# A graph network on one core: node rows spread from 32 nodes of a chunk instead of 128, one edge projection for k and v, sums joined per window

## The chip, the cores and the metric

The kernel runs on one core of a Trainium2 chip. Its time is the device time of one execution in microseconds; the median of 11 executions is 7646.16 us (7627.25 to 7656.26). The engines named below are PE (matrix products, with PEld for its weight loads), DVE (vector), ACT (scalar), POOL (GpSimd, here the issuer of the gathers) and SP (the issuer of most other DMAs).

## What is computed

A graph of 6,250 nodes and 206,250 edges, sorted by target node. First one message layer: each edge takes its target's features and 16 edge features, and the node averages the messages. Then three attention layers over the same edges with 32 edge features. Cut to the core:

```python
# message layer, on h = relu(layernorm(x))
msg  = relu(concat(h[dst], edge_attr_16) @ W1 + b1)
x    = x + relu(segment_sum(msg, dst) / max(count, 1) + h @ Wres + bres)
# three attention layers, starting from h = relu(layernorm(x)); two heads of 32, two of 32, one of 64
q, k, v = h @ Wq + bq, h @ Wk + bk, h @ Wv + bv
e     = edge_attr_32 @ We                       # the same e for k and for v
alpha = sum(q[dst] * (k[src] + e)) / sqrt(C)
a     = softmax of alpha over the edges of one dst
h     = segment_sum(a * (v[src] + e), dst) + h @ Ws + bs   # PReLU after the first two
# at the end x + h
```

## The kernel before

The edges are padded to 404 chunks of 512 (`CH`); a window is four chunks, 2,048 edges in 16 tiles of 128, and there are 101 windows (`NW`). Because edges are sorted by target, a window touches at most 128 neighbouring nodes, counted from its first node (`base`). A check of the target list at the start chooses between this program (`windows`) and a general one that handles any list; with these inputs `windows` runs.

*Spreading a node's row to its edges.* PE multiplies a transposed one-hot (`ohT`, 128 nodes by the edges of a tile, bf16) with the rows of the window's 128 nodes. To keep 32-bit precision the rows are cut into three bf16 parts (`parts`), and there are three matmuls for each tile that add up in PSUM.

*Summing edges into nodes.* PE multiplies a one-hot (`oh`, edges by 128 nodes, f32, made on DVE by comparing a row of indices with the edge's local node `dl`) with the messages, into one PSUM tile `acc` per window. The first node of a window can be the last of the window before; a matmul with `last` as weights adds the earlier window's sum of it (L339, L532).

*The graph stage* (L302 to L366) goes window by window: it loads edge features (eight DMAs for four windows, L311), the local node numbers (`lb`, L315) and the node rows (`q`, L317), makes `ohT` on DVE and also writes it to DRAM (`ohd`, L321) for the layers; projects the edges (L325), spreads the rows (L329), applies the activation (L333), makes one-hots (L336), sums (L340), and then normalises the nodes and projects them for the first attention layer (`project`), which stores k and v (L261), q with the skip row (L262) and the node features (L352).

*A layer* (`attention`) goes chunk by chunk. `fetch` (L383) gathers the k and v rows of 512 edges by four indirect DMAs on POOL, four chunks ahead. `load` brings a window's edge features (four DMAs, L391), its `ohT` and its `q`, one window ahead. `scores` projects the edges (L415, 512 columns: e stands twice, for k and for v), spreads q (L419, 12 matmuls of a chunk), adds e to k and v (L421), multiplies (L423) and reduces (L425). When a group of four windows (`ST` = 64 tiles) has its scores, `rows`, `chain` and `columns` find the maxima by scans and the exponentials. `sums` follows some 18 chunks behind: weights times v (L524), one-hots (L529), sums (L533), and at the end of a window `done` divides, adds the skip row and calls `project` for the next layer. What is left of `sums` after a layer's last gather is called the drain below; the gathers of the next layer need all of its k and v rows.

*Order.* A scheduler orders the instructions of each engine; each engine then works in that order. A DMA whose DRAM address depends on a window's first node needs a register load from SBUF on SP first (`first_node`, L234). The DMAs of SP and ACT take eight completion semaphores in turn, and an issue waits until the DMA that had its semaphore before has landed. Most pools have two or three buffers; PSUM tiles two.

Of the kernel before, what the change touches and what calls it, by code (L numbers as in the profile page):

```python
# [30 lines left out]
P = 128  # L31
# [15 lines left out]
WC = WT // 4  # L47
NR = NP + P
# [5 lines left out]
QW = 96 + D  # L54
# [10 lines left out]
def gnn_kernel(ctx: ExitStack, tc: tile.TileContext, x, src_t, dst_t, dst_row, ea16, ea32, eaT16, eaT32, w, out):  # L65
# [25 lines left out]
    base_i = cp.tile([1, NW], I32, name="base_i")  # L91
    base = cp.tile([P, NW], F32, name="base")
    with tc.tile_pool(name="chk", bufs=1) as p, tc.tile_pool(name="chkp", bufs=1, space=PSUM) as pp:
# [4 lines left out]
        ends = p.tile([NW, 2], F32, name="ends")  # L98
# [3 lines left out]
        nc.vector.tensor_copy(ends[:, 0:1], cur[:, 0:1])  # L102
        nc.vector.tensor_copy(ends[:, 1:2], after)
        nc.vector.memset(ends[0:1, 0:1], 0.0)
        bad = p.tile([NW, 2], F32, name="bad")
        fall = p.tile([NW, WE], F32, name="fall")
        nc.vector.tensor_tensor(fall, prev, cur, op=OP.is_gt)
        nc.vector.tensor_reduce(bad[:, 0:1], fall, axis=AX.X, op=OP.add)
        span = p.tile([NW, 1], F32, name="span")
        nc.vector.tensor_sub(span, ends[:, 1:2], ends[:, 0:1])  # L110
        nc.vector.tensor_single_scalar(bad[:, 1:2], span, float(P - 1), op=OP.is_gt)
        ones = p.tile([NW, P], F32, name="ones")
        nc.vector.memset(ones, 1.0)
        pb = pp.tile([P, NW], F32, name="pb")
        nc.tensor.matmul(pb, ends[:, 0:1].to_broadcast([NW, P]), ident[:NW, :NW], start=True, stop=True)
        nc.vector.tensor_copy(base, pb)
        nc.vector.tensor_copy(base_i, pb[0:1, :])
        pbad = pp.tile([P, 2], F32, name="pbad")
# [6 lines left out]
        nc.vector.tensor_scalar(lb, cur, ends[:, 0:1], None, op0=OP.subtract)  # L125
# [13 lines left out]
def windows(ctx: ExitStack, tc, x, src_t, dst_t, eaT16, eaT32, w, out, ident, w0, wl, slope, lrow, starts, base_i,  # L139
# [6 lines left out]
    qt = [dr.tile([NR, QW + D if l == 0 else QW], F32, name=f"qt{l}") for l in range(LAYERS + 1)]  # L146
# [3 lines left out]
    ohd = dr.tile([NW, P, WE], BF16, name="ohd")  # L150
# [10 lines left out]
    pidx = iota([P, 1], "pidx", [[0, 1]], 1)  # L161
    one = cp.tile([1, P], F32, name="one")
# [19 lines left out]
    for l in range(LAYERS):  # L182
        t = cp.tile([P, 8 * D], F32, name=f"wblk{l}")
        nc.gpsimd.memset(t, 0.0)
        for j in range(4):
            for i in range(2):
                nc.scalar.dma_start(t[j * 32:(j + 1) * 32, (2 * j + i) * D:(2 * j + i + 1) * D], w[f"L1_gnn_We{l}"])
        wblk.append(t)
    srci = cp.tile([P, T], I32, name="srci")
    nc.sync.dma_start(srci, src_t)  # L190

    dl = cp.tile([P, NW, WT], F32, name="dl")
    step = cp.tile([P, NW], F32, name="step")
    last = cp.tile([P, NW], F32, name="last")
    nc.vector.tensor_sub(step[:, :NW - 1], base[:, 1:], base[:, :NW - 1])
    nc.vector.tensor_scalar(last[:, :NW - 1], step[:, :NW - 1], pidx[:, 0:1], None, op0=OP.is_equal)
    with tc.tile_pool(name="dsti", bufs=1) as p:
        dsti = p.tile([P, NW, WT], I32, name="dsti")
        nc.sync.dma_start(dsti, dst_t.rearrange("p (w t) -> p w t", t=WT))
        nc.vector.tensor_tensor(dl, dsti, base[:, :, None].to_broadcast([P, NW, WT]), op=OP.subtract)  # L200
# [32 lines left out]
    def first_node(wi):  # L233
        return nc.values_load(base_i[0:1, wi:wi + 1], engines=(SP,), min_val=0, max_val=NP,  # L234
                              skip_runtime_bounds_check_because="a node")

    def parts(wp, q, dest):

        k = len(q.shape) - 1
        at = lambda i: dest[(slice(None),) * k + (slice(i * D, (i + 1) * D),)]  # L240
# [6 lines left out]
    def project(wp, mp, h, l, wi):  # L247
# [9 lines left out]
        q = wp.tile([P, QW], F32, name="q_n")  # L257
        parts(wp, po[:, :D], q[:, :96].bitcast(BF16))
        nc.scalar.copy(q[:, 96:], po[:, 3 * D:])
        at = first_node(wi)  # L260
        nc.sync.dma_start(kvt[l + 1][bass.ds(at, P), :], kv)  # L261
        nc.sync.dma_start(qt[l + 1][bass.ds(at, P), :], q)  # L262


    with tc.tile_pool(name="n0", bufs=1) as pool, tc.tile_pool(name="n0w", bufs=2) as wp, \
# [17 lines left out]
        rows = pool.tile([P, NB + 1, QW + D], F32, name="rows")  # L283
        nc.gpsimd.memset(rows[:, NB, :], 0.0)
        nc.gpsimd.tensor_copy(rows[:, :NB, QW:], xs)
        for b0 in range(0, NB, 4):
# [10 lines left out]
            parts(wp, po[:, :nb, :D], rows[:, b0:b0 + nb, :96].bitcast(BF16))  # L297
            nc.vector.tensor_copy(rows[:, b0:b0 + nb, 96:QW], po[:, :nb, D:])
        nc.sync.dma_start(qt[0].rearrange("(b p) f -> p b f", p=P), rows)


    with tc.tile_pool(name="g0", bufs=2) as gp, tc.tile_pool(name="e0", bufs=3) as ep, \  # L302
# [3 lines left out]
        for wi in range(NW):  # L306
# [7 lines left out]
            lb = gp.tile([P, WE], BF16, name="lb0")  # L314
            nc.sync.dma_start(lb, lrow[None, wi * WE:(wi + 1) * WE].to_broadcast([P, WE]))  # L315
            q = gp.tile([P, QW + D], F32, name="q0")
            nc.sync.dma_start(q, qt[0][bass.ds(first_node(wi), P), :])  # L317
            qb = q[:, :96].bitcast(BF16)
            ohT = gp.tile([P, WE], BF16, name="ohT0")
            nc.vector.tensor_scalar(ohT, lb, pidx[:, 0:1], None, op0=OP.is_equal)  # L320
            nc.scalar.dma_start(ohd[wi], ohT)  # L321
            acc = pp.tile([P, D + 1], F32, name="acc0")
            for u in range(2):
                pm = pp.tile([P, 8 * D], F32, name="pm")
                nc.tensor.matmul(pm, ea[:, wi % 4, u, :], w0blk, start=True, stop=False)  # L325
                for j in range(8):
                    t = u * 8 + j
                    for s in range(3):
                        nc.tensor.matmul(pm[:, j * D:(j + 1) * D], ohT[:, t * P:(t + 1) * P], qb[:, s * D:(s + 1) * D],  # L329
                                         start=False, stop=(j == 7 and s == 2))  # L330
# [3 lines left out]
                oh = ep.tile([P, 8, P], F32, name="oh0")  # L334
                for j in range(8):
                    nc.vector.tensor_scalar(oh[:, j, :], row, dl[:, wi, u * 8 + j:u * 8 + j + 1], None, op0=OP.is_equal)  # L336
                for j in range(8):
                    if wi > 0 and u == 1 and j == 7:
# [808 lines left out]
```

## Time and profile before

| | us |
|---|---|
| median of 11 executions | 7646.16 |
| profiled execution, its own time | 7659.01 |
| its span, first to last instruction | 7657.0 |
| PE busy (share of the span) | 5775.8 (75%) |
| POOL busy | 4756.8 (62%) |
| DVE busy | 4230.1 (55%) |
| ACT busy | 908.7 (12%) |
| mean granted PE clock | 0.733 |
| mean share of the DMA engines | about 0.35 in the layers, 0.43 in the graph stage |

Stages by the trace: start until 219 us, graph stage 219 to 1265, first gather at 1277.5, layers to 3340.3, 5469.3 and 7596.8 (last gather's end), each followed by a drain of 60 to 68 us. In the views, a group's line has the line of the code, the engine, the operation, out<-in with shapes and the count, then busy us and the mean ns of one, then the engine's idle us just before them and what ended most of that. A timeline's line has start us, duration us, engine (SPq and ACTq are DMA issues), line, operation and count, and in brackets the idle time before and its releaser. A line of waits has total us, times and the longest.

### The profile page before, as it was taken

How to read it: one execution, taken by the hardware profiler on the slowest of the kernel's cores; microseconds unless marked ns; L12 is line 12 of the kernel's file. 1: busy time of each engine (PE TensorE's matmuls, PEld its weight loads, DVE VectorE, ACT ScalarE, POOL GpSimd, SP SyncE). 2: the span in 40 equal slices, each digit the busy share in tenths (PEclk: the TensorE clock that was granted, in tenths of full speed). 3: DMA queues.
4: the chain of work that ended last, by engine and by line, in shares of the span. 5: the costliest groups of instructions: out<-in, count | busy, mean ns of one | idle time of the engine just before them, and what ended most of it. 6: DMA issues, size and time to landing. Idle time of an engine off the chain costs nothing. (4 is left out here: it accounts for less than half of the span.)

```text
span 7657.0 us, 121925 instructions
## 1 busy us (share of the span) xinstructions
PE 5775.8 (75%) x38234; PEld 4059.7 (53%) x38234; DVE 4230.1 (55%) x16431; ACT 908.7 (12%) x4161; POOL 4756.8 (62%) x5246
## 2 busy tenths in 40 slices
PE   1898887777777877776787777778767778777777
PEld 1676665555555555454554555555545555555555
DVE  2565455555555555554555555555545555555555
ACT  1232221011111111110111111111100000000000
POOL 0000002777777777747777777777477777777775
PEclk9998887677766677856768777776666776666676
DMA  1543434333333333323333333333233333333332
GB/s 34 184 158 129 137 129 124 99 101 103 101 104 101 100 104 102 101 71 100 100 105 101 102 103 101 104 102 100 70 100 97 101 97 98 99 96 98 99 96 73
DMA packets 680405, 789.19 MB, mean 103 GB/s; under 512 B 256945, under 2 KB 536851, under 8 KB 679517
## 3 DMA queue, kind: packets, MB, share of 16 engines
q1 hardware_dynamic: 507928, 408.61, 17.6%
q0 software_dynamic: 155136, 318.03, 14.8%
q10 hardware_dynamic: 16687, 54.66, 1.9%
q8 instruction: 309, 5.06, 0.3%
q14 instruction: 345, 2.83, 0.1%
HBM read 669.72 MB, written 112.64 MB: 102 GB/s over the span
## 5 line engine op out<-in xcount | busy, mean ns | idle before, releaser
L383 POOL DMA_INDIRECT kv<-kvt,srci x4848 | 4687.9, 967 | 1511.2 <-issue 1164.3
L415 PE MATMUL pe<-wblk,ea 128*128 128x512 f32 x2424 | 2008.3, 923 | 1355.2 <-DVE kv L421 1287.6
L533 PE MATMUL acc<-u,oh 128*128 128x66 f32 (+1 forms) x9696 | 2145.0, 359 | 138.2 <-DVE oh L529 106.1
L421 DVE TENSOR_TENSOR kv<-kv,pe 128x512 f32<-128x512 f32 x1212 | 832.0, 687 | 2401.7 <-DMA kv<-kvt,srci 2113.2
L533 PEld LDWEIGHTS acc<-u,oh 128*128 128x128 f32 x9696 | 1884.4, 267 | 251.5 <-DVE oh L529 113.1
L419 PEld LDWEIGHTS <-ohT 128*128 128x128 bf16 x14544 | 1004.1, 127 | 1074.2 <-issue 867.3
L415 PEld LDWEIGHTS pe<-wblk,ea 128*128 128x128 f32 x2424 | 495.3, 254 | 1501.2 <-DVE kv L421 1254.7
L529 DVE TENSOR_SCALAR oh<-row,dl 128x128 f32<-128x128 f32 x4848 | 1126.4, 290 | 8.4 <-PE acc L533 8.2
L419 PE MATMUL pq<-q,ohT 128*128 128x64 bf16 x14544 | 1028.5, 226 | 14.8 <-DMA q<-qt 10.3
L332 POOL MEMSET msg<- 128x8 f32 x202 | 22.7, 113 | 1039.3 <-PE acc L340 899.5
L524 DVE TENSOR_TENSOR u<-kv,ex 128x256 f32<-128x256 f32 x1212 | 505.4, 417 | 5.5 <-issue 2.9
L336 DVE TENSOR_SCALAR oh<-row,dl 128x128 f32<-128x128 f32 x1616 | 380.1, 281 | 232.2 <-PE acc L340 196.7
L425 DVE TENSOR_REDUCE al<-prod 128x8 f32<-128x256 f32 (+1 forms) x1212 | 497.6, 411 | 1.3
L423 DVE TENSOR_TENSOR prod<-kv,pq 128x256 f32<-128x256 f32 x1212 | 493.7, 408 | 5.2 <-DVE kv L421 0.5
L340 PEld LDWEIGHTS acc<-msg,oh 128*128 128x128 f32 x3232 | 429.7, 205 | 107.9 <-issue 73.0
L523 ACT COPY u<-ex 128x8 f32<-128x8 f32 (+1 forms) x1212 | 235.1, 201 | 2113.7 <-PE acc L533 2095.8
L340 PE MATMUL acc<-msg,oh 128*128 128x65 f32 x3232 | 455.0, 290 | 29.6 <-ACT msg L333 13.7
L325 PE MATMUL pm<-w0blk,ea 128*128 128x512 f32 x404 | 253.8, 725 | 25.9 <-DMA ea<-in_eaT_dram 25.9
L254 PE MATMUL po<-wl,ht 65*128 65x256 f32 x606 | 247.9, 497 | 8.4 <-ACT ht L252 8.0
L329 PEld LDWEIGHTS <-ohT 128*128 128x128 bf16 x4848 | 188.0, 103 | 94.5 <-issue 68.3
L329 PE MATMUL pm<-q,ohT 128*128 128x64 bf16 x4848 | 191.8, 198 | 43.6 <-DMA q<-qt 40.1
L552 ACT COPY win<-acc 128x66 f32<-128x66 f32 (+1 forms) x303 | 65.3, 215 | 1311.2 <-PE acc L533 1308.2
(156 smaller groups left out, 2988.5 us busy)
## 6 DMA issues: line engine op xcount, KB each, us to landing
ohT<-ohd SPq DMA_DIRECT2D x303, 512.0 KB
ea<-in_eaT_dram SPq DMA_DIRECT2D x1412, 64.0 KB
kv<-kvt,srci POOLq DMA_INDIRECT x4848
lb<-lrow SPq DMA_DIRECT2D x101, 512.0 KB
ohd<-ohT ACTq DMA_DIRECT2D x101, 512.0 KB
qt<-q_n SPq DMA_DIRECT2D x303, 80.0 KB
kvt<-kv_n SPq DMA_DIRECT2D x303, 64.0 KB
q<-qt SPq DMA_DIRECT2D x303, 48.0 KB
```

The costliest lines, as they stand in the source:

```text
L329: nc.tensor.matmul(pm[:, j * D:(j + 1) * D], ohT[:, t * P:(t + 1) * P], qb[:, s * D:(s + 1) * D], start=False, stop=(j == 7 and s == 2))
L336: nc.vector.tensor_scalar(oh[:, j, :], row, dl[:, wi, u * 8 + j:u * 8 + j + 1], None, op0=OP.is_equal)
L340: nc.tensor.matmul(acc, oh[:, j, :], msg[:, j, :], start=(u == 0 and j == 0), stop=(u == 1 and j == 7))
L383: nc.gpsimd.indirect_dma_start(out=t[:, j, :], out_offset=None, in_=kvt[l + 1][:, :], in_offset=bass.IndirectOffsetOnAxis(ap=srci[:, 4 * c ...
L415: nc.tensor.matmul(pe.rearrange("p j f -> p (j f)"), ea[:, k, :], wblk[l], start=True, stop=True)
L419: nc.tensor.matmul(pq[:, j, :], ohT[:, (4 * k + j) * P:(4 * k + j + 1) * P], q[:, i * D:(i + 1) * D], start=(i == 0), stop=(i == 2))
L421: nc.vector.tensor_add(kv, kv, pe)
L423: nc.vector.tensor_mul(prod, kv[:, :, :D], pq)
L425: nc.vector.tensor_reduce(als[s][:, :, t0:t0 + 4].rearrange("p h j -> p j h"), prod.rearrange("p j (h c) -> p j h c", h=H), axis=AX.X, op= ...
L524: nc.vector.tensor_mul(u[:, :, :D].rearrange("p j (h c) -> p j h c", h=H), kv[:, :, D:].rearrange("p j (h c) -> p j h c", h=H), e[:, :, :, ...
L529: nc.vector.tensor_scalar(oh[:, j, :], row, dl[:, wi, 4 * k + j:4 * k + j + 1], None, op0=OP.is_equal)
L533: nc.tensor.matmul(acc, oh[:, j, :], u[:, j, :], start=(k == 0 and j == 0), stop=(k == WC - 1 and j == 3))
```

## The change

In words:

- The node rows are spread from the 32 nodes (`CN`) that a chunk of 512 edges can touch, not from the 128 of a window. The three bf16 parts of these 32 nodes are stacked into 96 partitions, so that one matmul per tile does what three did. The rows of a window are loaded by four DMAs, one per chunk, each with its own first node (`load_q`); `base`, `dl` and the local numbers are kept per chunk.
- The node table is split: bf16 parts (`qt`) and f32 rows for the skip and the residual (`st`), stored and loaded apart.
- The edge projection is done once per chunk, with 256 columns, and added to k and v by one DVE operation that reads it twice.
- The one-hots of the sums have 32 columns and are made by one DVE operation per chunk (in the graph stage one per eight tiles); each chunk's sums go to its own 32 rows of `acc`, and `nodes` joins them per 128 nodes: a copy, a one-hot from `slot`, a matmul and a second copy. The last tile of the first chunk and the carried row are added in the second chunk's turn.
- The edge features of the layers are laid out once, DRAM to DRAM, by four DMAs per window on ACT's queue in the graph stage (`ead`); a layer then loads them by one DMA instead of four.
- `ex` and `sc` have four buffers instead of two.

```diff
+CN = 32
...
+    qt = [dr.tile([NR, 3, D], BF16, name=f"qt{l}") for l in range(LAYERS + 1)]
+    st = [dr.tile([NR, 2 * D if l == 0 else D], F32, name=f"st{l}") for l in range(LAYERS + 1)]
...
+    ohd = dr.tile([NW, 3 * CN, WE], BF16, name="ohd")
+    ead = dr.tile([NW, P, WC, P], F32, name="ead")
...
+    slot = cp.tile([P, NW], F32, name="slot")
+    for c in range(WC):
+        r = slice(c * CN, (c + 1) * CN)
+        nc.vector.tensor_sub(slot[r, :], base[r, :, c], base[r, :, 0])
+    nc.vector.tensor_scalar(slot, slot, pmod[:, 0:1], None, op0=OP.add)
...
         at = first_node(wi)
         nc.sync.dma_start(kvt[l + 1][bass.ds(at, P), :], kv)
-        nc.sync.dma_start(qt[l + 1][bass.ds(at, P), :], q)
+        nc.sync.dma_start(qt[l + 1][bass.ds(at, P)], q)
+        nc.sync.dma_start(st[l + 1][bass.ds(at, P), :], skip)
+
+    def load_q(pool, l, wi):
+        q = pool.tile([3 * CN, WC, D], BF16, name="q")
+        for c in range(WC):
+            at = first_node(wi, c)
+            nc.sync.dma_start(q[:, c, :], qt[l][bass.ds(at, CN)].rearrange("n i f -> (n i) f"))
+        return q
+
+    def nodes(wp, mp, acc, wi, F):
+        s = wp.tile([P, F], F32, name="sums")
+        nc.scalar.copy(s, acc)
+        of = wp.tile([P, P], F32, name="of")
+        nc.vector.tensor_scalar(of, row, slot[:, wi:wi + 1], None, op0=OP.is_equal)
+        pn = mp.tile([P, F], F32, name="pn", tag="m")
+        nc.tensor.matmul(pn, of, s, start=True, stop=True)
+        win = wp.tile([P, F], F32, name="win", bufs=3)
+        nc.scalar.copy(win, pn)
+        return win
...
-        nc.sync.dma_start(qt[0].rearrange("(b p) f -> p b f", p=P), rows)
+        nc.sync.dma_start(qt[0].rearrange("(b p) i f -> p b i f", p=P), q)
+        nc.scalar.dma_start(st[0].rearrange("(b p) f -> p b f", p=P), rows)
...
+            for j in range(4):
+                nc.scalar.dma_start(
+                    ead[wi, j * 32:(j + 1) * 32],
+                    eaT32[:, wi * WE:(wi + 1) * WE].rearrange("k (c j e) -> k c j e", j=4, e=P)[:, :, j])
+            lb = gp.tile([3 * CN, WE], BF16, name="lb0")
+            nc.sync.dma_start(lb, lrow[None, wi * WE:(wi + 1) * WE].to_broadcast([3 * CN, WE]))
+            q = load_q(gp, 0, wi)
+            rx = gp.tile([P, 2 * D], F32, name="rx")
+            nc.sync.dma_start(rx, st[0][bass.ds(first_node(wi), P), :])
...
-                    for s in range(3):
-                        nc.tensor.matmul(pm[:, j * D:(j + 1) * D], ohT[:, t * P:(t + 1) * P], qb[:, s * D:(s + 1) * D],
-                                         start=False, stop=(j == 7 and s == 2))
+                    nc.tensor.matmul(pm[:, j * D:(j + 1) * D], ohT[:, t * P:(t + 1) * P], q[:, t // 4, :],
+                                     start=False, stop=(j == 7))
...
-                oh = ep.tile([P, 8, P], F32, name="oh0")
-                for j in range(8):
-                    nc.vector.tensor_scalar(oh[:, j, :], row, dl[:, wi, u * 8 + j:u * 8 + j + 1], None, op0=OP.is_equal)
+                oh = ep.tile([P, 8, CN], F32, name="oh0")
+                nc.vector.tensor_tensor(oh, row[:, None, :CN].to_broadcast([P, 8, CN]),
+                                        dl[:, wi, u * 8:(u + 1) * 8, None].to_broadcast([P, 8, CN]), op=OP.is_equal)
...
             ea = gp.tile([P, WC, P], F32, name="ea")
-            for j in range(4):
-                nc.sync.dma_start(
-                    ea[j * 32:(j + 1) * 32],
-                    eaT32[:, wi * WE:(wi + 1) * WE].rearrange("k (c j e) -> k c j e", j=4, e=P)[:, :, j])
+            nc.sync.dma_start(ea, ead[wi])
...
-            pe = pp.tile([P, 4, 2 * D], F32, name="pe")
+            pe = pp.tile([P, 4, D], F32, name="pe")
...
-                for i in range(3):
-                    nc.tensor.matmul(pq[:, j, :], ohT[:, (4 * k + j) * P:(4 * k + j + 1) * P], q[:, i * D:(i + 1) * D],
-                                     start=(i == 0), stop=(i == 2))
-            nc.vector.tensor_add(kv, kv, pe)
+                nc.tensor.matmul(pq[:, j, :], ohT[:, (4 * k + j) * P:(4 * k + j + 1) * P], q[:, k, :],
+                                 start=True, stop=True)
+            both = kv.rearrange("p j (i f) -> p j i f", i=2)
+            nc.vector.tensor_add(both, both, pe[:, :, None, :].to_broadcast([P, 4, 2, D]))
...
-            oh = ep.tile([P, 4, P], F32, name="oh")
-            for j in range(4):
-                nc.vector.tensor_scalar(oh[:, j, :], row, dl[:, wi, 4 * k + j:4 * k + j + 1], None, op0=OP.is_equal)
+            oh = ep.tile([P, 4, CN], F32, name="oh")
+            nc.vector.tensor_tensor(oh, row[:, None, :CN].to_broadcast([P, 4, CN]),
+                                    dl[:, wi, 4 * k:4 * k + 4, None].to_broadcast([P, 4, CN]), op=OP.is_equal)
+            if k == 1:
+                if wi > 0:
+                    nc.tensor.matmul(acc[0:1, :], last[:, wi - 1:wi], carried(wi, s, g), start=False, stop=False)
+                nc.tensor.matmul(acc[:CN, :], *state["late"], start=False, stop=True)
             for j in range(4):
-                if wi > 0 and k == WC - 1 and j == 3:
-                    nc.tensor.matmul(acc[0:1, :], last[:, wi - 1:wi], carried(wi, s, g), start=False, stop=False)
-                nc.tensor.matmul(acc, oh[:, j, :], u[:, j, :], start=(k == 0 and j == 0),
-                                 stop=(k == WC - 1 and j == 3))
+                if k == 0 and j == 3:
+                    state["late"] = oh[:, j, :], u[:, j, :]
+                    continue
+                nc.tensor.matmul(acc[k * CN:(k + 1) * CN, :], oh[:, j, :], u[:, j, :], start=(j == 0), stop=(j == 3))
...
-            win = st["win"] = wp.tile([P, F], F32, name="win", bufs=3)
-            nc.scalar.copy(win, acc)
+            win = state["win"] = nodes(wp, mp, acc, wi, F)
```

The graph stage has the same order of sums (`late`, the carried row, 32 rows per chunk) and the same join as the layers.

## The prediction

> **What bounds the kernel now.** I read the engines' busy time by stage first, then the costliest groups, POOL's own timeline, and SP's timeline in the first stage. The views by stage give, for a stretch, each engine's busy us (count), the granted clock, the DMA share and GB/s, in the order PE, PEld, DVE, ACT, POOL:
>
> ```profile
> 219.00:1265.00 1046.00, 900.70 (x8965) 706.27 (x8965) 577.15 (x2894) 282.16 (x998) 22.52 (x199) 0.89 0.43 144
> 1277.50:3340.30 2062.80, 1567.01 (x9634) 1073.56 (x9635) 1201.34 (x4481) 224.74 (x1144) 1574.23 (x1668) 0.72 0.35 102
> 3340.30:3408.00 67.70, 51.74 (x208) 42.92 (x209) 36.77 (x182) 11.51 (x61) 0.85 (x5) 0.53 0.15 36
> ```
>
> The kernel is one graph stage (101 windows, 1046 us, 10.36 us each), three attention layers of about 2061 us, and a drain after each of them (67.7, 67.5 and 60.2 us). In the graph stage PE is busy 86%: PE bounds it. In a layer both PE and POOL show 76%, so busy shares don't decide; the groups and POOL's timeline do.
>
> ```profile
> L383 POOL DMA_INDIRECT kv<-kvt,srci x4848 | 4687.9, 967 | 1511.2 <-issue 1164.3
> L421 DVE TENSOR_TENSOR kv<-kv,pe 128x512 f32<-128x512 f32 x1212 | 832.0, 687 | 2401.7 <-DMA kv<-kvt,srci 2113.2
> L529 DVE TENSOR_SCALAR oh<-row,dl 128x128 f32<-128x128 f32 x4848 | 1126.4, 290 | 8.4 <-PE acc L533 8.2
> ```
>
> ```profile
> 2309.16 0.95 POOL L383 DMA_INDIRECT kv<-kvt,srci  x1 [0.30 <-DVE oh L529]
> 2310.41 0.95 POOL L383 DMA_INDIRECT kv<-kvt,srci  x1 [0.30 <-issue]
> 2311.66 0.95 POOL L383 DMA_INDIRECT kv<-kvt,srci  x1 [0.30 <-issue]
> ...
> 3339.36 0.95 POOL L383 DMA_INDIRECT kv<-kvt,srci  x1 [0.30 <-issue]
> 3395.91 0.30 POOL L451 MEMSET b<- 1x260 f32 x1 [55.61 <-DVE wins L546]
> ...
> 3408.01 0.95 POOL L383 DMA_INDIRECT kv<-kvt,srci  x1 [11.24 <-DMA kvt<-kv_n]
> ```
>
> POOL issues a gather every 1.25 us, with the same 0.30 us between them whoever is named as releaser; it never waits longer inside a layer. 1616 gathers x 1.25 = 2020 us of the layer's 2061. The first DVE work of each chunk waits 2113 us in all for gathers to land, and PE waits for that DVE work. So POOL's gather rate bounds the layers; PE and DVE have slack there. Only in the drains, where POOL is idle, does PE pace again: 38.5 of 67.7 us are the sums of L533.
>
> **The change part by part.**
>
> *Attention, matmuls (L415, L419).* Per chunk the edge projection goes from 512 columns to 256 and the query spread from 12 matmuls to 4: 1004 us of L415 and 8/12 x 1028 = 686 us of L419 leave PE. The gathers cover them; they are worth 0. That cover is not gone anywhere except in the drains, which hold almost none of these rows.
>
> *Attention, one-hots (L529).* Four TENSOR_SCALARs of 290 ns become one TENSOR_TENSOR of the same 128 elements per lane (nearest: 128x128 f32 TENSOR_TENSOR L495, 273 ns); 850 us leave DVE, hidden as well. But the gather itself moves: fastest 941 ns, median 947, mean 967, so 4848 x 20 ns = 97 us lie above the median, and in the undisturbed first 60 us of the second layer, with no L529 running, the rows all show 0.94 or 0.95. Ends: 0 (the new one-hot, or L524, disturbs as much) and -97. I take -60, since L524 runs on unchanged.
> By the Trainium skill, "SBUF — State Buffer", section "Who interferes with whom", a tensor_scalar can lock a port pair that GpSimd needs for its descriptors, while tensor_tensor has no such mode, though with two SBUF inputs it contends with a GpSimd instruction that reads SBUF. By the first half alone the term would be about -97, by the second it could be near 0; the row of 967 against 947 fits either.
>
> *Attention, sums and the new join.* 16 matmuls with 128-wide weights become 16 with 32-wide weights, plus the copy of sums (ACT, as L552, 215 ns), a one-hot (DVE, 290) and one 128-wide matmul and a second copy. Under the gathers: 0. In a drain it counts:
>
> ```profile
> 3392.45 6.64 PE L533 MATMUL acc<-u,oh 128*128 128x66 f32 x30 [0.39 <-ACT u L523]
> 3399.02 0.38 PE L532 MATMUL acc<-wins,last 128*1 128x66 f32 x2
> ```
>
> 30 records take 6.57 us from start to start, 219 ns each; the one with a single weight column takes 155 (3399.02 to 3399.33). A 32-wide one lies between, nearer the latter if loading goes by columns: about 165. A drain holds 160 of them: 160 x 0.054 = 8.6 us less. Against it each of six windows gets two hops more, some 1 us (copy 0.2, join 0.3, copy 0.2 and the handovers), and the row carried from the window before is now wanted in the second chunk instead of the last, so PE, which works in order, has only the six records of the first chunk (1.0 us) to run meanwhile. Net -5 per drain, between 0 and -10; three drains: -15 (0 to -30). The deeper rings for ex and sc can only help here; I give them nothing.
>
> *Start.* The node table goes out as 384-byte rows on SP and 512-byte rows on ACT instead of one 896-byte row: twice the pieces. The old one is issued at 195.84 and lets work begin at 214.4: 18.5 us. Ends: 0 (the same bytes, almost) and +25 (twice the pieces, and other small set-up steps); I take +13.
>
> *Graph stage.* PE loses two thirds of L329 (192 us) and part of L340 (453 us): 128 us and about 453 x (1 - 105/118) = 50 us, where 118 and 105 ns are the start-to-start spacings of wide and single-column sums at full clock. 1046 - 178 leaves 868 us, 8.6 per window: PE stops being alone. DVE loses more than it gets (16 x 280 ns go, two of about 410 and one of 290 come). What is added is issuing. SP's timeline in this stage:
>
> ```profile
> 604.28 0.37 SPq L262 DMA_DIRECT2D qt<-q_n  x1
> 605.17 0.33 SPq L352 DMA_DIRECT2D x1t<-x  x1
> 606.07 0.36 SPq L317 DMA_DIRECT2D q<-qt  x1
> 606.48 0.42 SPq L311 DMA_DIRECT2D ea<-in_eaT_dram  x1
> ```
>
> A DMA whose address is a node read from SBUF comes 0.89 us after the one before; a plain one 0.41 to 0.47. Before, a window has three node reads (q, x1t, kvt) and four plain issues (qt, lb, two of ea): 3 x 0.89 + 4 x 0.45 = 4.5 us. After: seven node reads (four chunks' q, rx, x1t, kvt) and five plain (qt, st, lb, two ea): 6.2 + 2.25 = 8.5 us. That is a floor of 101 x 8.5 = 858 us, about PE's. On top come waits in order on SP:
>
> ```profile
> SPq L261 <- ACT q_n L241: 236.5, 91, 7.4
> SPq L262 <- DVE q_n L245: 79.5, 90, 2.5
> ```
>
> The stores (L261, L262) wait 2.3 and 0.8 us per window; behind them on SP stand the loads for the next windows, for which PE waits. The first mostly vanishes when SP itself is late; the second stays, because L262 follows L261 by 0.4 us and its data need two more steps. I add 0.9 us: 9.4 us per window, 949 us, -97. ACT gets four issues per window for the edge copy (0.43 each by the like loads on SP, L311) and one more copy: 2.8 + 0.33 + 1.7 + 0.2 = 5.0 of 9.4 us. Each issue also waits until the DMA that had its completion semaphore, eight issues back over both queues, has landed (the built program's order shows it); at 17 DMAs per window instead of 8 this ties ACT's computing to SP's pace. Ends: -190 (floors reached, nothing else) and +170 (12 us per window by such ties).
> By the Trainium skill, "DMA: Bandwidth & Descriptors", section "Specifications", pieces under 512 B fall below line rate because of a read-modify-write; the new q rows are 128 B. It gives no price; the trace before has 384-byte q rows only, so nothing here shows it. It speaks for the upper end.
>
> *Sum* against the profiled run's own time: 7659.0 + 13 - 97 - 60 - 15 = 7500. That run is 12.9 us over the median of the eleven shown, so 7490 on their scale.
>
> **The rivals** (on the median's scale, 7646).
> 1. *The floor is reached*: 8.5 us per window, -188 in the graph stage: 7400. For it: loads have two buffers, so SP can run ahead. Against: SP also holds the stores, in order.
> 2. *Slower: the issue queues take PE's place with more than PE had.* SP's node reads and ACT's DMA issues, tied by the completion semaphores, stretch a window. It decides from 1046 + 62 = 1108 us, 11 us per window. At 12 us: +166 + 13 - 75 = 7750. For it: ACT carries a serial chain (sums, join, normalisation, projection) and each of its five DMA issues may stop it for a landing; a stored row that is 0.5 us late on ACT holds SP. Against: SP waits 4.5 us per window before (the two rows above and 142.9 us of L352 for DVE), so it has room to be late.
> 3. *The graph stage stays at 10.4 us* by the serial chain of steps per window, and only gathers and drains gain: 7646 + 13 - 75 = 7584.
> 4. *PE bounds the layers after all*: about 2 us per chunk would go (0.83 + 0.57 + 0.5), 1212 x 2 = 2400 us, 5200. Against: the even 1.25 us of POOL.
>
> **How the numbers follow.** Forecast 0.45, rival 1 0.24, rival 2 0.15, rival 3 0.12, rival 4 0.02; the rest (about nothing, sums that cancel) 0.02. The range leaves out rival 4, the far part of rival 1 and most of rival 2: 7340 (forecast with -190, -97, -30, +13 is 7342) to 7680. 0.2% is 15 us, about what this kernel's runs can tell from no change. Faster 0.81, within it 0.05, slower 0.14.
>
> **What would show it.** Right: gathers 1.25 us apart from first to last of each layer, each layer between 2030 and 2055 us, mean gather 950 to 960 ns; SP in the graph stage issuing almost without a pause, PE under 75% there at a clock above 0.89; a window of 9 to 10 us; drains of 55 to 65 us. Wrong: a gather interval other than 1.25, POOL waiting for kv buffers in a layer, long waits of ACT or SP for landed DMAs in the graph stage, or drains that grow by the join.

## The result, and the profile after

The changed kernel takes 7904.49 us (median of 8 executions, 7898.14 to 7911.72), the kernel before 7645.14 us (31 executions). The ratio is 1.0339, with an interval of 1.0329 to 1.0349: slower by 3.4%, where the forecast was 7490 us and faster. The profiled execution spans 7901.7 us, before 7657.0.

The views by stage for the changed kernel (busy us and count of PE, PEld, DVE, ACT, POOL, then the granted clock, the DMA share and GB/s): the graph stage, the first layer, the drain after it.

```profile
240.00:1615.45 1375.45, 800.37 (x5957) 479.61 (x5957) 421.73 (x1614) 302.85 (x1111) 22.74 (x199) 0.69 0.38 106
1615.45:3665.50 2050.05, 1247.84 (x6588) 853.84 (x6588) 994.65 (x3415) 245.18 (x1238) 1561.45 (x1666) 0.50 0.36 96
3665.50:3717.00 51.50, 34.01 (x223) 24.67 (x224) 28.14 (x131) 13.18 (x68) 1.34 (x7) 0.50 0.15 26
```

Place by place, in the profiled executions:

| | before | after | difference | forecast |
|---|---|---|---|---|
| first PE work of the graph stage | 220.4 | 240.4 | +20 | +13 |
| from there to the first gather | 1057 | 1375 | +318 | -97 |
| three layers, first to last gather | 2062.8, 2061.3, 2060.0 | 2050.1, 2048.5, 2043.6 | -42 | -60 |
| three drains | 67.7, 67.5, 60.2 | 51.5, 49.5, 43.1 | -51 | -15 |
| sum | | | +245 | -159 |

The differences add up to the 244.7 us between the spans. The whole loss lies in the graph stage: a window takes 13.6 us in place of 10.5 (1375 and 1057, each by 101). No engine is full there. PE, 86% busy before, is 58% busy (800 of 1375 us), and its granted clock fell from 0.89 to 0.69.

In the costliest groups of the changed kernel the gather is still the bound of the layers, with the same 0.30 us after nearly each ("issue" ends most of its idle time), and DVE's first work of a chunk still waits for it:

```profile
L442 POOL DMA_INDIRECT kv<-kvt,srci x4848 | 4646.9, 959 | 1514.2 <-issue 1170.4
L475 DVE TENSOR_TENSOR kv<-kv,pe 128x512 f32<-128x512 f32 x1212 | 832.9, 687 | 3053.5 <-DMA kv<-kvt,srci 2948.0
L582 DVE TENSOR_TENSOR oh<-row,dl 128x128 f32<-128x128 f32 x1212 | 339.6, 281 | 5.8 <-PE acc L592 3.2
```

What holds the graph stage shows on SP. Its waits there in the changed kernel (us in total, times, longest):

```profile
SPq L411 <- DVE m L413: 234.4, 78, 6.1
SPq L287 <- ACT q_n L266: 106.6, 70, 4.5
SPq L288 <- DVE q_n L270: 48.7, 71, 3.1
```

The three lines are the window's stores: x1 (L411), k and v (L287), q (L288). Before, the store of x1 waited less (the lines of the other two, L261 and L262, stand in the forecast):

```profile
SPq L352 <- DVE m L354: 142.9, 36, 11.0
```

Behind the stores, on the same queue, stand the loads of the next windows. SP's timeline over one window (1013.0 to 1030.0 us):

```profile
1014.15 0.36 SPq L288 DMA_DIRECT2D qt<-q_n  x1
1014.73 0.33 SPq L289 DMA_DIRECT2D st<-skip_n  x1
1015.11 0.43 SPq L369 DMA_DIRECT2D lb<-lrow  x1
1016.11 0.35 SPq L296 DMA_DIRECT2D q<-qt  x1
1019.89 0.37 SPq L411 DMA_DIRECT2D x1t<-x  x1
1020.77 1.97 SPq L296 DMA_DIRECT2D q<-qt  x3
1023.73 0.35 SPq L372 DMA_DIRECT2D rx<-st  x1
1024.63 0.37 SPq L287 DMA_DIRECT2D kvt<-kv_n  x1
```

One q load goes out at 1016.11. Then SP stands until the store of x1 can go (1019.89), and only after it come the other three q loads. From 240 to 1600 us all of SP's waits in the profile sum to 467 us, 4.7 us per window. What is left of a window, 8.9 us, I take for issuing. The spacings in this timeline, 0.81 to 0.90 us before an issue with a node read and 0.38 to 0.59 us before a plain one, give 7.6 to 9.3 us for seven and five of them. That is the floor of 8.5 us of the forecast, nearly as worked out; the waits on top of it are 4.7 us and not 0.9.

PE feels it at its first matmul of a window, the edge projection, before the change and after:

```profile
L325 PE MATMUL pm<-w0blk,ea 128*128 128x512 f32 x404 | 253.8, 725 | 25.9 <-DMA ea<-in_eaT_dram 25.9
L380 PE MATMUL pm<-w0blk,ea 128*128 128x512 f32 x404 | 309.9, 874 | 172.7 <-DMA ea<-in_eaT_dram 125.5
```

It stood idle 25.9 us for the edge features, which SP loads, and now 125.5 us; its waits for q went from 40.1 to 54.9 us. The same matmul also takes 874 ns instead of 725, at a granted clock of 0.69 instead of 0.89.

### The profile page after: what moved, and what is told of

It is laid out like the page before. It is cut to its first block, busy times and chain, and to the rows that moved or that the text cites. A ratio compares the mean times of both kernels' runs of the same rounds, so it can differ in the third digit from the quotient of the medians.

```text
span 7901.7 us, 99343 instructions
## 1 busy us (share of the span) xinstructions
PE 4512.4 (57%) x26120; PEld 3055.0 (39%) x26120; DVE 3427.0 (43%) x11804; ACT 993.4 (13%) x4565; POOL 4715.3 (60%) x5248
## 5 line engine op out<-in xcount | busy, mean ns | idle before, releaser
L442 POOL DMA_INDIRECT kv<-kvt,srci x4848 | 4646.9, 959 | 1514.2 <-issue 1170.4
L469 PE MATMUL pe<-wblk,ea 128*128 128x256 f32 x2424 | 1438.7, 697 | 2209.2 <-DVE kv L475 1752.9
L592 PE MATMUL acc<-u,oh 128*32 128x66 f32 (+1 forms) x9090 | 1255.0, 314 | 209.3 <-DVE oh L582 199.0
L592 PEld LDWEIGHTS acc<-u,oh 128*32 128x32 f32 x9090 | 930.2, 164 | 391.1 <-DVE oh L582 282.8
L472 PEld LDWEIGHTS <-ohT 96*128 96x128 bf16 x4848 | 480.9, 138 | 455.0 <-issue 343.5
L472 PE MATMUL pq<-q,ohT 96*128 96x64 bf16 x4848 | 529.1, 245 | 13.9 <-DMA q<-qt 9.8
L380 PE MATMUL pm<-w0blk,ea 128*128 128x512 f32 x404 | 309.9, 874 | 172.7 <-DMA ea<-in_eaT_dram 125.5
L582 DVE TENSOR_TENSOR oh<-row,dl 128x128 f32<-128x128 f32 x1212 | 339.6, 281 | 5.8 <-PE acc L592 3.2
L306 PE MATMUL pn<-sums,of 128*128 128x65 f32 (+1 forms) x808 | 250.7, 409 | 72.4 <-ACT sums L302 72.1
L400 PE MATMUL acc<-msg,oh 128*32 128x65 f32 x3030 | 225.9, 265 | 103.3 <-ACT msg L387 80.9
L306 PEld LDWEIGHTS pn<-sums,of 128*128 128x128 f32 x808 | 197.7, 292 | 173.4 <-ACT sums L302 141.9
L400 PEld LDWEIGHTS acc<-msg,oh 128*32 128x32 f32 x3030 | 186.0, 136 | 168.4 <-issue 136.0
```

Of the source, the lines that this page charges most:

```text
L306: nc.tensor.matmul(pn, of, s, start=True, stop=True)
L400: nc.tensor.matmul(acc[c * CN:(c + 1) * CN, :], oh[:, j, :], msg[:, j, :], start=(j % 4 == 0), stop=(j % 4 == 3))
L442: nc.gpsimd.indirect_dma_start(out=t[:, j, :], out_offset=None, in_=kvt[l + 1][:, :], in_offset=bass.IndirectOffsetOnAxis(ap=srci[:, 4 * c ...
L469: nc.tensor.matmul(pe.rearrange("p j f -> p (j f)"), ea[:, k, :], wblk[l], start=True, stop=True)
L472: nc.tensor.matmul(pq[:, j, :], ohT[:, (4 * k + j) * P:(4 * k + j + 1) * P], q[:, k, :], start=True, stop=True)
L582: nc.vector.tensor_tensor(oh, row[:, None, :CN].to_broadcast([P, 4, CN]), dl[:, wi, 4 * k:4 * k + 4, None].to_broadcast([P, 4, CN]), op=OP ...
```

## The experiments

Theory A: SP's queue, its issue time and its waits in order together, sets the window. Theory B: ACT with its new DMA issues, and the completion semaphores that SP and ACT share. Theory C: the longer chain of steps by the join. The runs came in four groups. In the second and third (e5 to e12) the kernel before takes 9710 and 9714 us, and gathers pause, mostly for 2 to 9 us after every 8 to 20 of them. What brings the pauses stays open: the third and the fourth group carry the same chip number, and the fourth has none. The graph stage is the same there (where only the layers are changed, in e7, e8 and e12, it ends at 1617, 1609 and 1620 us, against 1615 in the changed kernel), so of these runs I use the graph stage and comparisons inside a group. A time without a range is one execution. The first gather of one and the same graph stage differs by up to 14 us between runs (e6 and e10 below), so a smaller difference tells nothing.

**e1: the copy of the edge features goes.**

```diff
-            for j in range(4):
-                nc.scalar.dma_start(ead[wi, j * 32:(j + 1) * 32], eaT32[...][:, :, j])
...
-            nc.sync.dma_start(ea, ead[wi])
+            for j in range(4):
+                nc.sync.dma_start(ea[j * 32:(j + 1) * 32], eaT32[...][:, :, j])
```

> The changed kernel without the edge copy: the four DRAM-to-DRAM issues per window leave ACT's queue in the graph stage, and the layers load the edge features by four DMAs per window as before. The graph stage of the changed kernel takes 13.5 us per window (first gather at 1615 us). Theory A (SP's queue bounds it: 12 issues and 7 node reads per window, 8.5 us, plus in-order waits of some 4.5 us): SP keeps all of that, the first gather moves by 0 to 60 us, time 7840 to 7900. Theory B (ACT's DMA issues and the shared completion semaphores stretch the window): 17 DMAs per window become 13, window back to 10 or 11 us, first gather near 1300, time 7580 to 7650.

7948.53 us (before: 7644.74 in this group). The first gather comes at 1580.5, 35 us earlier. ACT's 404 issues and the semaphores that they take were worth 35 of the 338 us by which the first gather had moved; theory B falls as the main cause. What this run lost it lost in the layers: 2085.6, 2082.6 and 2050.8 us, with a mean gather of 974 ns against 959.

**e2: the q loads at fixed addresses.** Still four DMAs per window on SP, of the same size, but without a node read.

```diff
-            q = load_q(gp, 0, wi)
+            for c in range(WC):
+                nc.sync.dma_start(q[:, c, :], qt[0][c * CN:(c + 1) * CN].rearrange("n i f -> (n i) f"))
```

> The changed kernel with the graph stage's four q loads per window at fixed addresses (the table's first 128 rows, so the first layer's messages are those of wrong nodes): same DMAs, same bytes, but 4 of 7 node reads per window are gone from SP. Theory A: 4 x 0.45 us of SP per window, 11.7 us per window, 180 us less: 7720. Theory B: issues and landings are the same, so 7890 to 7905. Theory C (the serial chain of a window's steps, not SP's time, sets the window): less than 60 us gain, 7850 to 7900.

7686.85 us, first gather at 1393.4: 222 us earlier. SP's timeline of this run has the four loads at 0.43 to 0.48 us each, in the changed kernel three of them took 1.97 us:

```profile
803.06 0.43 SPq L369 DMA_DIRECT2D lb<-lrow  x1
803.59 1.77 SPq L372 DMA_DIRECT2D q<-qt  x4
805.87 0.37 SPq L374 DMA_DIRECT2D rx<-st  x1
```

The quickest spacings in the stage before an issue are 0.81 us with a node read and 0.41 without (tenth percentiles of q, changed kernel and e2), so 404 loads became cheaper by some 164 us, and the stage shortened by 222; SP's waits became shorter as well (last table of this section).

**e3: the q loads on POOL**, which is idle in the graph stage.

```diff
-            q = load_q(gp, 0, wi)
+            for c in range(WC):
+                at = nc.values_load(base_i[0:1, wi, c:c + 1], engines=(mybir.EngineType.Pool,), ...)
+                nc.gpsimd.dma_start(q[:, c, :], qt[0][bass.ds(at, CN)].rearrange("n i f -> (n i) f"))
```

> The changed kernel with the graph stage's q loads, node reads included, issued by POOL, which is idle there; four reads and four issues per window leave SP and no q load stands behind a store any more. Theory A: SP's own work falls from 8.5 to 5 us per window and its waits overlap better, window 9.5 to 10.5 us, 300 to 400 us less: 7500 to 7600. Theory B: still 17 DMAs, but only 13 on the shared semaphores, partial gain, 7700. Theory C: under 100 us gain, 7800 to 7900.

7499.35 us, against 7644.74 before: the first gather at 1213.8, 402 us earlier than in the changed kernel and 64 earlier than before the change. POOL issues such a load every 0.94 us (its timeline: 0.51 us and 0.43 after it):

```profile
810.91 0.51 POOL L374 DMA_DIRECT2D q<-qt  x1 [0.42 <-issue]
811.85 0.51 POOL L374 DMA_DIRECT2D q<-qt  x1 [0.43 <-issue]
```

So a node read costs POOL no less than SP; what changed is whose queue it stands in. Layers (2045.0, 2048.9, 2045.5) and drains (49.6, 49.7) are those of the changed kernel. Theory A holds. This run takes both from SP, the issue time of the q loads and their place behind the stores, and doesn't tell the two apart; e2 takes part of the issue time alone.
The Trainium skill, "Perfetto Trace Analysis", section "DMA Optimizations", says that balancing DMAs among SP, ACT and GpSimd may help where their issuing is the bottleneck. These runs agree with it (402 us by e3); in e5 and e15 below a further load on GpSimd made it slower.

**e4: no join in the graph stage.**

```diff
-            win = nodes(wp, mp, acc, wi, D + 1)
+            win = wp.tile([P, D + 1], F32, name="win0", bufs=3)
+            nc.scalar.copy(win, acc)
```

> The changed kernel without the join per 128 nodes in the graph stage: the sums are copied once and used as they lie (so each node's sums are wrong there), two hops of the serial chain (matmul pn and a second copy, 1.2 us by the trace) are gone. Theory A: SP's wait for the store of x1t shrinks by about that, 100 to 130 us less, 7775 to 7800. Theory C: the chain is what bounds a window, 1.2 us of 13.5 and what PE does idle with it, 120 to 250 us less, 7650 to 7780. Theory B: under 50 us, 7850 to 7900.

7914.85 us, first gather at 1621.9, no earlier than with the join. Theory C, the join's steps as what sets the window, falls.

**e5: the loads of lb and rx on POOL too** (e3, and `nc.gpsimd` for L369 and L372).

> The changed kernel with all loads of the graph stage's node data (q, rx and the local numbers lb, with their node reads) issued by POOL; SP keeps the stores and the edge features. With q alone on POOL the run gave 7499 us, first gather at 1214. Theory A (what stands behind a store on SP is late): no load but ea stands behind a store now, window from 9.7 to 8.5-9.2 us, 50 to 120 us less: 7380 to 7450. Rival A2 (with q off SP the queue is no longer the bound; PE and the chain are): within 25 us of the former, 7475 to 7525. Rival A3 (POOL's own issue, about 1.25 us for each of six loads, and its waits for buffers in order, become the new queue): slower, 7530 to 7600.

9285.86 us; first gather at 1354.0, 140 us later than in e3. POOL's queue seems to have taken SP's place: it stood 146.4 us before the load of `lb` until a result of DVE was there. No run tests this further.

**e6 and e10: e3 with three buffers** for the loads of the graph stage.

```diff
-    with tc.tile_pool(name="g0", bufs=2) as gp, ...
+    with tc.tile_pool(name="g0", bufs=3) as gp, ...
```

> The changed kernel with the graph stage's q loads on POOL and three buffers instead of two for its loaded tiles. Theory A2/C (loads run too little ahead): window 9.7 to about 9.0 us, 50 to 90 us less, 7410 to 7450. If depth is not what is missing: 7480 to 7515.

> The changed kernel with the four q loads of a window on POOL and three buffers instead of two for the loads of the graph stage. Theory A, that SP's queue held the graph stage: first gather between 1155 and 1215 us (1214 with two buffers), layers as in the changed kernel (about 2047 each), drains about 50, 50 and 43: 7450, between 7435 and 7500, which is 0.97 to 0.98 of the kernel before. If three buffers bring nothing on this chip: 7500.

9107.33 us in the second group; in the third 9083.58 (4 executions, 9079.43 to 9106.99), a ratio of 0.9357 (0.9339 to 0.9375) to the kernel before there. The times of 7435 to 7500 could not come out on these chips; the first gather, at 1164.8 and 1151.0, is 49 to 63 us earlier than with two buffers. With the q loads off SP, a deeper buffer helps.

**e13: three buffers alone**, q on SP as in the changed kernel (run in the fourth group, whose kernel before takes 7649.41).

> The changed kernel with three buffers instead of two for the loads of the graph stage (ea, lb, q, rx, ohT); all queues as in the changed kernel. Theory A1, SP's issue time and its waits in order set the window: deeper buffers let nothing be issued sooner on a full queue, first gather within 40 us of 1615. Theory A5, the q loads wait for their buffer: as with the q loads on POOL, where three buffers brought 50 to 60 us, or more: first gather at 1500 to 1565 us.

7892.81 us, first gather at 1597.5, 18 us earlier, little more than runs differ by. The buffers weren't what held the q loads; SP's waits stayed nearly as they were:

```profile
SPq L411 <- DVE m L413: 218.7, 75, 6.0
SPq L287 <- ACT q_n L266: 97.3, 68, 4.0
SPq L288 <- DVE q_n L270: 48.4, 70, 3.1
```

**e9: the store of x1 on ACT**, the one that SP waits for longest.

```diff
-            nc.sync.dma_start(x1t[bass.ds(first_node(wi), P), :], x1)
+            at = nc.values_load(base_i[0:1, wi, 0:1], engines=(mybir.EngineType.Activation,), ...)
+            nc.scalar.dma_start(x1t[bass.ds(at, P), :], x1)
```

> The changed kernel with one edit: the store of x1 into x1t (L411) is issued by ACT, not by SP; the q loads stay on SP. Theory A2, it is the waiting of that store on SP that holds up the q loads behind it: 234 us of waits and 101 node reads of 0.89 us leave SP, about 320 us; the first gather comes at about 1295 us and the time is about 7585. Theory A1, only the time of issuing counts and the wait moves on to the next store (L287): 90 us, first gather at about 1525, time about 7815. Theory A4, ACT, which has the serial chain of a window, pays for the issue and the wait itself: first gather within 40 us of 1615, time about 7900.

9469.0 us; first gather at 1542.6: 73 us earlier, near the 90 of theory A1 and far from the 320 of theory A2. The waits tell why. L411 is gone from SP's list, and the wait has moved to the next store:

```profile
SPq L287 <- ACT q_n L266: 283.1, 79, 8.1
SPq L288 <- DVE q_n L270: 49.8, 50, 2.2
```

L287 went from 106.6 to 283.1 us. What left SP for good is the time of the issue (8.9 to 8.1 us a window in the last table). (A caution for this and the other moves: the scheduler orders the engines anew for each kernel.)

**e11 and e14: both**, q on POOL with three buffers and the store of x1 on ACT.

> The kernel with the q loads on POOL and three buffers, and the store of x1 on ACT as well. If SP's queue still sets the pace of the graph stage there: another 50 to 90 us, first gather at 1080 to 1115 us, time about 7380. If PE (70% busy at a clock of 0.8) and the chain of steps of a window set it: within 20 us of the same kernel with the store on SP. If ACT becomes the bound by the issue: 30 to 60 us slower than that one.

> The kernel with the q loads on POOL, three buffers and the store of x1 on ACT once more. First gather between 1070 and 1090 us; layers of about 2047 us each where gathers run 1.25 us apart throughout; time about 7380, a ratio of 0.965 to the kernel before. Where gathers also pause (as in the last two groups of runs): ratio 0.926, as there.

In the third group 9001.23 us (8985.0 to 9015.61), ratio 0.926 (0.924 to 0.9279). In the fourth 7376.03 us (4 executions, 7370.43 to 7382.43) against 7649.41, ratio 0.9645 (0.9629 to 0.9662), first gather at 1085.4 (1079.9 in e11). This is the best version, 3.5% faster than the kernel before and 6.7% faster than the changed one (7376.03 / 7904.49). Its view by stage within the graph stage, its group of the edge projection, and its gather group:

```profile
300.00:1000.00 700.00, 515.86 (x4919) 314.10 (x4915) 336.10 (x1391) 238.10 (x916) 196.57 (x507) 0.87 0.64 181
```

```profile
L384 PE MATMUL pm<-w0blk,ea 128*128 128x512 f32 x404 | 268.9, 754 | 123.1 <-ACT msg L391 88.7
L448 POOL DMA_INDIRECT kv<-kvt,srci x4848 | 4648.0, 959 | 1503.3 <-issue 1165.2
```

PE is 74% busy again, at a clock of 0.87; a window takes 8.4 us. What its edge projection waits for most is now a result of ACT, no longer the loads of SP. The layers are untouched (959 ns a gather, 2049.8, 2050.5 and 2042.9 us).

**e15: the load of rx on POOL as well.**

> The same with the load of rx on POOL as well, so that SP has two node reads per window (kvt, and the stores beside it) and four plain issues. If SP's issue time still sets the window, 0.9 us times 101 at a slope of 0.8 to 1.2 as in the runs before: 70 to 110 us faster than e14. If PE and the chain of steps set it: within 20 us of e14. If POOL's queue, where loads stand behind waits for free q buffers, makes rx late: 20 to 100 us slower.

7445.17 us (7431.42 to 7453.39), ratio 0.9733 (0.9713 to 0.9753): 69 us slower than e14 in the same group, first gather at 1157.2. POOL's waits are longer before the fill of `msg` (each line of it was at most 33 us in e14), and a wait at the load of `rx` is new:

```profile
POOL msg L392 <- ACT q_n L269: 134.9, 53, 5.3
POOL rx L378 <- DVE m L422: 76.3, 83, 1.4
```

SP issues less here than in any other row of the table below, and the stage is longer than in e14, so SP's issue time is no longer the price. By these rows another queue in order, POOL's, has become it; no run tests that.

**e7 and e12: wide sums in the layers again**, the rings for ex and sc left deep.

```diff
-            oh = ep.tile([P, 4, CN], F32, name="oh")
-            nc.vector.tensor_tensor(oh, ...)
+            oh = ep.tile([P, 4, P], F32, name="oh")
+            for j in range(4):
+                nc.vector.tensor_scalar(oh[:, j, :], row, dw[:, wi, 4 * k + j:4 * k + j + 1], None, op0=OP.is_equal)
...
-                nc.tensor.matmul(acc[k * CN:(k + 1) * CN, :], oh[:, j, :], u[:, j, :], ...)
+                nc.tensor.matmul(acc, oh[:, j, :], u[:, j, :], ...)
...
-            win = state["win"] = nodes(wp, mp, acc, wi, F)
+            nc.scalar.copy(win, acc)
```

> The changed kernel with the sums of the layers as before (four one-hots of 128 columns per chunk by TENSOR_SCALAR, one accumulation over the window's 128 nodes, no join); deeper rings for ex and sc stay. The changed kernel's drains are 51.5, 49.5 and 43.1 us, before 67.7, 67.5 and 60.2. Theory D1 (narrow sums shorten the drains): drains back to 64-68, 64-68 and 57-61, and with gathers at 967 ns again about +36 us in the layers: 7980 to 8000. Rival D2 (the deeper rings do): drains stay at 48 to 54 us, 7930 to 7950.

> The changed kernel with the sums of the attention layers over 128 nodes again (four one-hots of 128x128 by TENSOR_SCALAR, 16 matmuls into acc of 128 rows, no join); the deeper rings for ex and sc, the query spread and the shared edge projection stay. Theory D1, narrow sums shorten the drains: drains of 62 to 70 us instead of 51.5, 49.5 and 43.1. Theory D2, the deeper rings or the smaller spread do it: 45 to 55. For the gathers: if the wide one-hots are what stretched them, the mean gather goes from 959 ns to about 967, which is 40 us over the three layers; if not, it stays within 2 ns of 959. Time about 7905 plus 30 to 50 us if D1, plus 0 to 40 if D2.

9532.79 and 9535.16 us. The drains are 80.4 and 80.4, and again 80.4 and 80.3; in e9, which has the narrow sums and ran in the group of e12, they are 62.2 and 64.0, 16 to 18 us less. In the group of e7 the first two drains of e5, e6 and e8, with narrow sums, are 62.2 to 72.6, which is 8 to 18 us less. So the narrow sums shorten a drain, by 8 to 18 us where gathers pause; the change shortened them by 16.2, 18.0 and 17.1. The deeper rings, which e7 and e12 keep, don't do it alone. PE's timeline in a drain, of the changed kernel and then of e12:

```profile
3676.22 2.53 PE L592 MATMUL acc<-u,oh 128*32 128x66 f32 x24
```

```profile
4197.68 1.90 PE L589 MATMUL acc<-u,oh 128*128 128x66 f32 x8
```

24 narrow records in 2.53 us, the last of 0.32, are 96 ns apart ((2.53 - 0.32) / 23; 106 and 110 in two shorter rows of this drain); 8 wide ones in 1.90 us, the last of some 0.38, are 217 ns apart. The gather takes 963 ns in e12 and 959 in e9: wide one-hots in the old form would explain some 4 of the 8 ns between 967 and 959. Width and form change together there, and one kernel run twice (e6, e10) has 957 and 960 ns.

**e8: four TENSOR_SCALARs for the one-hots, still 32 wide.**

```diff
-            nc.vector.tensor_tensor(oh, row[:, None, :CN].to_broadcast([P, 4, CN]), dl[...], op=OP.is_equal)
+            for j in range(4):
+                nc.vector.tensor_scalar(oh[:, j, :], row[:, :CN], dl[:, wi, 4 * k + j:4 * k + j + 1], None, op0=OP.is_equal)
```

> The changed kernel with the layers' one-hots of 32 columns made by four TENSOR_SCALARs per chunk instead of one TENSOR_TENSOR. Theory G1 (the form of the DVE instruction disturbs the gathers): mean gather from 959 to 965-970 ns, layers 2060, 30 to 45 us more, 7930 to 7950. Rival G2 (something else, such as the number of DMAs that SP issues beside them: with four edge loads per window they took 981 ns in the first two layers): gathers stay at 957 to 961 ns, 7890 to 7915.

9628.38 us. The gather groups of e8 and of e6, from the same group of runs:

```profile
L442 POOL DMA_INDIRECT kv<-kvt,srci x4848 | 4614.6, 952 | 3175.0 <-DVE u L578 1491.8
```

```profile
L446 POOL DMA_INDIRECT kv<-kvt,srci x4848 | 4641.8, 957 | 3123.6 <-issue 1282.0
```

952 ns with TENSOR_SCALARs, 957 without: that form doesn't stretch the gathers here.

**Over all runs**: SP's window, split by the sum of its waits in the profile (taken over the graph stage, per window) and the rest, which is issuing. The window is (first gather - 240) / 101.

| | window, us | SP waits | the rest |
|---|---|---|---|
| before (from 220) | 10.5 | 5.7 | 4.8 |
| changed | 13.6 | 4.7 | 8.9 |
| e13, three buffers | 13.4 | 4.5 | 8.9 |
| e9, x1 on ACT | 12.9 | 4.8 | 8.1 |
| e2, fixed addresses | 11.4 | 4.0 | 7.4 |
| e3, q on POOL | 9.6 | 4.6 | 5.0 |
| e14, both, three buffers | 8.4 | 3.9 | 4.4 |
| e15, rx on POOL too | 9.1 | 5.9 | 3.2 |

Waits and rest add up to the window in any kernel, so the table alone doesn't show that SP sets it; e2, e3, e9 and e14 do, where less on SP makes the window shorter. From before to the changed kernel the issuing rises by 4.1 us, and the waits give back only 1.0 of it; from there to e14 the issuing falls by 4.5 and the waits by 0.8. The waits are hardly slack: SP waits for the stores of a window, whose chain waits for loads that SP has to issue first (PE for `ea` 125.5 us and for `q` 54.9 us in the changed kernel). Only in e15 does this end: the issuing falls once more, SP's waits grow, and the window with them.

## Why the prediction was wrong

**The step that failed** is in the graph stage: "The first mostly vanishes when SP itself is late ... I add 0.9 us: 9.4 us per window, 949 us, -97." The waits came to 4.7 us and the window to 13.6; the term is +318, not -97. Of the 404 us between the forecast sum and the profiled time (7500 against 7903.4), 415 are this term; the others make up for 11. The working before it stood: 0.81 to 0.90 us for an issue with a node read, 0.38 to 0.59 for a plain one, a floor of 8.5 us (8.9 measured as the rest beside the waits). I treated SP's waits as slack that a late SP uses up. The store of k and v did wait less (236.5 us on L261, now 106.6 on L287), but the store of x1 waits more (142.9 on L352, now 234.4 on L411), and that one I had named in a rival only and left out of the term. e9 shows the same trade the other way: the wait taken from L411 comes back at L287. All waits of SP together went only from 5.7 to 4.7 us a window. Some of the loss may pass through PE's clock, which the forecast saw rise: the same 128x512 matmul takes 725 ns before, 874 after and 754 in e14. No run holds the clock still, so this share stays open.

**Rival 2** (slower, the issue queues) is what happened, and its decision point of 11 us fits: e2 with 11.4 us is slower than before, e3 with 9.6 faster. Its price of 7750 was too low by 155 us, and its mechanism half right: SP, not ACT and not the semaphores (e1: 35 us). Its argument against, "so it has room to be late", was the same error. **Rival 1** (the floor reached) would need SP to run ahead of its stores; with the deeper buffers of e13 it didn't. **Rival 3** asked for a window that the chain of steps holds at 10.4 us; e3 and e14 run at 9.6 and 8.4. **Rival 4** falls: PE's busy time in the first layer fell by 319 us and the layer by 13, and a gather comes every 1.27 us in the mean (2050.05 / 1616), before every 1.28.

**Gathers.** Forecast -60, measured -41 in gather time (4687.9 to 4646.9) and -42 over the layers, inside the ends given. The reason given, one TENSOR_TENSOR in place of four TENSOR_SCALARs, isn't borne out: e8 puts the form back at 32 wide and gathers don't slow (952 against 957). Wide one-hots in that form account for some 4 of 8 ns (e12); the rest stays open, so the size came out near by luck in part. By the Trainium skill, "SBUF — State Buffer", section "Who interferes with whom", weighed in the forecast, the tensor_scalar form can lock GpSimd out. No run here shows that price at 32 columns, and e12 can't tell it from the width.

**Drains.** Forecast -5 each, measured -16 to -18. The mechanism, narrower weights on PE, was right in direction (e7 and e12). The mis-sized term is the record: estimated at 165 ns, measured 96 to 110, so 160 x (219 - 96) = 19.7 us, or 17.4 with 110, in place of 8.6. With 16 to 18 measured, nothing to 3.5 us are left for the hops that I put at 3.6 (8.6 - 5).

**Start.** Forecast +13, measured +20, inside the ends of 0 and +25.

**Layers.** Everything costed at nothing there, the edge projection, the spread, the one-hots and the join, was indeed hidden: PE's busy time in the first layer fell from 1567 to 1248 us and the layer by 13. (The 850 us that were to leave DVE were too many: 1126.4 less 1212 x 0.273 is 795, and 787 left, 1126.4 to 339.6.) The 128-byte pieces of q, set against the change by "DMA: Bandwidth & Descriptors", section "Specifications", are the same in e3, where the graph stage is shorter than before; they can't be what lengthened it. (Rows of 384 bytes were loaded in the layers only; those of the graph stage before had 896.)

**What would have shown it.** The window of 9 to 10 us, and a PE clock above 0.89 there, failed (13.6 and 0.69); SP "almost without a pause" failed with them. The drains, 43 to 52 us, were shorter than the 55 to 65 named.

## What to carry to other kernels

On an issue queue that holds both stores, which wait for results, and loads, which these results need, count issue time and waits together: the waits of the profile before stay when more issues are added. The added issues took 4.1 us of such a queue per window here (the four small loads with computed addresses alone take 3.3), more than the 1.8 us of matmul time that the forecast saw saved. On POOL's queue, nearly idle in that stage (22.7 us busy), these loads let the stage end 64 us earlier than before the change, and one load more made it later (e15). Before an engine is unloaded, work out what comes next on the queues, in the stage where it counts.

## What the runs showed that I had not expected

- PE's granted clock fell with its load: 0.89 at 86% busy (before), 0.69 at 58% (changed), 0.87 at 74% (e14), all in the graph stage. The Trainium skill, "TensorE: Matmul & The Clock Gate", section "Part 1: The HAM clock gate", says that the gate follows how busy PE has lately been, which agrees. The share of busy time alone doesn't give the clock, though: PE was 76% busy at 0.72 in a layer before. In the layers it fell from 0.72 to 0.50 and each layer still became shorter.
- Without the copy of the edge features (e1) the mean gather rises from 959 to 974 ns and the first two layers by 34 to 36 us each. The kernel before has the same four loads per window and 967 ns; why e1 is above it stays open.
